# Cross attention laid over the feed forward's 56 slots, stage by stage

## The chip, the cores and the metric

One core of one Trainium2 chip runs the kernel. The metric is device time in microseconds (us), from one launch to its end. All data is float32.

## The reference

A transformer layer pair. An encoder layer runs over a context of 77 tokens (batch 2); a decoder layer runs over 2 x 2048 tokens of width 512 with 16 heads of 32: causal self attention, cross attention into the 77 encoder tokens, and a feed forward of width 2048. Both attentions add a learned bias by relative position. Cut to what matters here:

```python
y = y + _mha(yn, yn, dec_sa_in_w, dec_sa_in_b, dec_sa_out_w, dec_sa_out_b, sb)
y = y + _mha(_ln(y, dec_n2_s, dec_n2_b), memory, dec_ca_in_w, dec_ca_in_b, dec_ca_out_w, dec_ca_out_b, cb)
h = _ln(y, dec_n3_s, dec_n3_b)
y = y + (jax.nn.relu(h @ dec_ff1_w.T + dec_ff1_b) @ dec_ff2_w.T + dec_ff2_b)
```

## The kernel before

The decoder's tokens are cut into 8 blocks of 512 (`blocks`, four for each batch entry), a block into 4 tiles of 128 tokens, t = 0 to 3. The kernel has two phases. In the first, self attention of all blocks runs, the encoder and the cross attention of block 0 mixed in between. It writes each block's rows to a buffer in device memory (`y1`). The second phase, which the change touches, does the feed forward of block x and, beside it, the cross attention of block x + 1.

**The feed forward.** Each of its two layers is cut into a 2 x 2 grid, and a product of the two grids is made from 7 products of sums and differences instead of 8 (`PARTS`, `ORDER`). Each of these is done in four quarters, so a block has 2 x 7 x 4 = 56 *slots*, `per` in the code: 28 of layer 1, then 28 of layer 2. `ff_slot(s)` first issues the operands of slot s + 3 (`prepare`, L1061: sums of weights and of inputs on GpSimd, sums of hidden values on VectorE in layer 2), then the matmuls of slot s: `first_product` (L1078) in layer 1, `second_product` (L1108) in layer 2. A slot is 4 float32 matmuls that the trace lists as 8. Four PSUM banks (4 to 7) take their results. In layer 1 VectorE copies them (L1090) or adds them (L1094) into the hidden values `kT`, ScalarE copies a part (L1092) and applies the relu (L1097). In layer 2 VectorE adds every fourth slot's result to the block's rows (L1116); finished rows are stored (L1121), and rows of the block after next are loaded into their place (`new_y`, L962).

**Cross attention.** `cross(x)` is a generator: it fills lists of functions, `plan`, and gives control back after each list. Four other PSUM banks, handed out in rotation by `bank()`, serve it. Its stages for a tile t, and the lines of their instructions:

- the second norm, three stages: statistics on VectorE (L699 to L701) with an inverse root on GpSimd (L702); centring on VectorE into `xt` (L708) and, on GpSimd, adding the output's bias to the residual rows (L709); transposes on TensorE (L714) with scale and shift alternating on VectorE (L720) and ScalarE (L718)
- the queries, four groups for all four tiles at once (L727, evicted at L728 on VectorE)
- `score`: 16 heads' products on TensorE (L741) into four banks, then maxima and differences on VectorE (L750, L751) into one buffer `pr`, the program's `oT`; where a bias is added (block 4's tiles 0 and 1), `bias` has loaded it into `pr` before (L106), and L748 adds it
- `exp` on ScalarE (L754)
- `normalize`: sum and reciprocal on VectorE (L759, L760), a multiply on GpSimd (L761)
- `turned`: 16 transposes on TensorE (L767) into the four banks, copied by ScalarE (L771) and VectorE (L769) in turn
- `times_v`: the product with the values (L778), copied by ScalarE into `xr` (L782)
- `out`: the output product (L787), added to the rows by VectorE (L788)
- the third norm, the same three stages as the second (L699 to L720), which writes the feed forward's input `nTt`

**What sets the order.** Every engine works through its own instructions in the order in which the program issues them, so a wait holds whatever stands behind it on that engine. The loop at the end issues, for each slot n, the lists of `plan` that are due, then `ff_slot`. Before the change `plan` has 32 lists, *steps*, spread over the 56 slots:

```python
while steps < n * 32 // per + 1:
    next(side, None)
    steps += 1
```

So step s comes ahead of slot ceil(1.75 s): steps 0, 1, 2, 3, 4 ahead of slots 0, 2, 4, 6, 7, and so on, every four steps seven slots. The first block's slots 0 to 7 have been done before this loop, so its steps there have no matmuls of the feed forward beside them. The last block has no cross attention beside it. Within a list the functions stand by tile, the earlier tile first.

Of the kernel before, what the change touches and what calls it, by code (L numbers as in the profile page):

```python
# [54 lines left out]
def tile_encoder_decoder(ctx: ExitStack, tc: tile.TileContext, ins, out):  # L55
# [22 lines left out]
    def vec(name, i):  # L78
        c = _COL[name] + i
        return vecs[:, c : c + 1]  # L80
# [18 lines left out]
    def bias_tile(dst, m, nq, nk, off):  # L99

        flat = tz[m].rearrange("h b t -> h (b t)")
        for r0 in range(0, nq, RB):
            n = min(RB, nq - r0)
            o = off - r0
            skew = flat[:, o : o + RB * (LT - 1)].rearrange("h (b u) -> b h u", u=LT - 1)
            nc.sync.dma_start(dst[r0 : r0 + n], skew[:n, :, :nk])  # L106
# [43 lines left out]
    with (  # L150
# [20 lines left out]
        def bank():  # L171

            i = count["bank"] % count["banks"]
            count["bank"] += 1
            return psum[:, i, :]
# [515 lines left out]
        def norm_stages(y, n, row, place, done):  # L691

            keep = {}

            def stats():
                st = sm.tile([P, 6], F32, name="bnst", tag="bnst")
                mv = sm.tile([P, 2], F32, name="cmv", tag="cmv", bufs=4)
                rs = sm.tile([P, 2], F32, name="crs", tag="crs", bufs=4)
                nc.vector.bn_stats(st, y())  # L699
                nc.vector.bn_aggr(mv, st)  # L700
                nc.vector.tensor_scalar_add(rs[:, 0:1], mv[:, 1:2], EPS)  # L701
                nc.gpsimd.tensor_tensor(rs[:, 1:2], rs[:, 0:1], mhalf[:, 0:1], ALU.pow)  # L702
                keep.update(mv=mv, rs=rs)

            def center():
                xn = keep["xn"] = place()
                mv, rs = keep["mv"], keep["rs"]
                nc.vector.tensor_scalar(xn, y(), mv[:, 0:1], rs[:, 1:2], ALU.subtract, ALU.mult)  # L708
                nc.gpsimd.tensor_tensor(y(), y(), row, ALU.add)  # L709

            def turned():
                xn, pt, dst = keep["xn"], bank(), done()
                for c in range(NC):
                    nc.tensor.transpose(pt[:, ts(c, P)], xn[:, ts(c, P)], ident)  # L714
                for c in range(NC):
                    sc, bi = vec(f"dec_{n}_s", c), vec(f"dec_{n}_b", c)
                    if c % 2:
                        nc.scalar.activation(dst[:, c, :], pt[:, ts(c, P)], AF.Identity, bias=bi, scale=sc)  # L718
                    else:
                        nc.vector.tensor_scalar(dst[:, c, :], pt[:, ts(c, P)], sc, bi, ALU.mult, ALU.add)  # L720

            return stats, center, turned

        def q_group(o, w, nT, dst):
            mm = bank()
            for c in range(NC):
                nc.tensor.matmul(mm, w[:, c, :], nT[:, c, :], start=(c == 0), stop=(c == NC - 1))  # L727
            nc.vector.tensor_scalar(dst, mm, vec("dec_ca_in_b", o), SCALE, ALU.add, ALU.mult)  # L728
# [138 lines left out]
        for x, (b, m) in enumerate(blocks):  # L867
# [14 lines left out]
            for t in range(TB):  # L882
                end = x == len(blocks) - 1
                jobs[u + NU + (2 if end else 7) + t].append(out_job(b, m, t))
                at = u + NU + ((-1, 0, 3, 4)[t] if end else 6 + t)
# [6 lines left out]
            for g in range(NC):  # L892
# [3 lines left out]
                at = u + g * TB - 3  # L896
# [48 lines left out]
        nT2 = vflat[:, 12 * D :].rearrange("p (c n) -> p c n", n=MB)  # L945
        pr = oT_all.rearrange("p a q -> p (a q)")[:, : H * S]
        kTcs = [pts_all[:, 4 + b, : NC * S].rearrange("p (c k) -> p c k", k=S) for b in range(B)]
        w_q, vcs, qT = [], [], []
# [7 lines left out]
        def y_of(x, t):  # L956
            return ys[x % 2][:, t, :]
# [177 lines left out]
        def ff_slot(s):  # L1135
            prepare(s + 3)
            (first_product if slots[s][1] == 1 else second_product)(s)

        def cross(x):

            b, m = blocks[x]
            plan = [[] for _ in range(32)]

            def place(tag):
                return lambda: sb.tile([P, D], F32, name=tag, tag=tag, bufs=3 if tag == "xt" else 2)

            def bias(t):
                bias_tile(pr.rearrange("p (h k) -> p h k", k=S), 2, P, S, 255 - P * t)

            for t in range(TB):  # L1150
                fs = norm_stages(
                    lambda t=t: y_of(x, t), "n2", bv, place("xt"), lambda t=t: nT2[:, :, ts(t, P)]
                )
                for k, f in enumerate(fs):
                    plan[t + k].append(f)
            for g in range(NC):
                plan[6 + g // 2].append(lambda g=g: q_group(g, w_q[g], nT2, qT[g // 2][:, g % 2, :]))
            for t in range(TB):
                at = 8 + 4 * t
                y = lambda t=t: y_of(x, t)  # L1160
                biased = m == 0 and t < 2
                if biased:
                    plan[at if t else at - 2].append(lambda t=t: bias(t))
                fs = attend_stages(
                    lambda g, t=t: qT[g // 2][:, g % 2, ts(t, P)], kTcs[b], vcs[b], y, biased, pr,
                    lambda g: pts_all[:S, g, :], place("xr"), wbt,
                )
                for k, f in zip((0, 1, 2, 4, 5, 6), fs):
                    plan[at + k].append(f)
                fs = norm_stages(y, "n3", bo, place("xt"), lambda t=t: nTt[:, :, ts(t, P)])  # L1170
                for k, f in enumerate(fs):
                    plan[at + 7 + k].append(f)
            for fs in plan:
                for f in fs:
                    f()
                yield
# [40 lines left out]
        per = len(slots) // len(blocks)  # L1217
        for x in range(len(blocks)):
            side = cross(x + 1) if x + 1 < len(blocks) else iter(())
            steps = 0  # L1220
            for n in range(per):
                while steps < n * 32 // per + 1:
                    next(side, None)
                    steps += 1
                if x or n >= 8:
                    ff_slot(x * per + n)

# [36 lines left out]
```

## Time and profile before

| | |
|---|---|
| median of 3 runs | 3166.06 us (3164.92 to 3169.56) |
| the profiled execution | 3163.36 us |
| its span, first to last instruction | 3161.5 us |
| mean granted TensorE clock | 0.978 of full |
| TensorE busy | 3007.3 us, 95% |
| VectorE busy | 2052.0 us, 65% |
| ScalarE busy | 1379.0 us, 44% |
| GpSimd busy | 740.8 us, 23% |
| the phase of the change | from about 1914 us to the end |

Shares of busy time are of the whole span, both phases. In the rows below, PE is TensorE's matmuls, PEld its weight loads, DVE VectorE, ACT ScalarE, POOL GpSimd and SP the engine that issues DMAs. A group or chain row names a line of the program (L1108), what is written and read, and a time. A row of waits reads: who waited, for whom, us in total, times, the longest. A row of windows reads: start and end, length, then busy time of PE, PEld, DVE, ACT and POOL with instruction counts, the granted TensorE clock (1.00 is full), the share of busy DMA engines and GB/s.

### The profile page before, as it was taken

What the parts mean: (1) busy time and instruction counts of PE and PEld (TensorE: products, weight loads), DVE (VectorE), ACT (ScalarE), POOL (GpSimd) and SP (SyncE); (2) the same over time, 40 slices, a digit from 0 to 9 for tenths busy, and PEclk for the clock granted to TensorE, in tenths of its full rate; (3) what the DMA queues carried; (4) which work ended last, traced back from release to release, by engine and by line L of the source; (5) the groups of instructions that cost most, each with busy time, mean ns of one, the idle gap of its engine ahead of it and who ended that gap; (6) DMA issues with size and microseconds to landing.
All of it is one profiled execution on the core that took longest, in us unless ns stands there. A gap on an engine that the chain in (4) does not pass through costs nothing. (4 is left out here: it accounts for less than half of the span.)

```text
span 3161.5 us, 60599 instructions
## 1 busy us (share of the span) xinstructions
PE 3007.3 (95%) x24328; PEld 2066.4 (65%) x24328; DVE 2052.0 (65%) x5859; ACT 1379.0 (44%) x2523; POOL 740.8 (23%) x601
## 2 busy tenths in 40 slices
PE   7899999999999999999999989999999899999999
PEld 4555566666665556666666656777777677777778
DVE  4765667766765777667666645566666666666665
ACT  3443456667775445566677752122121212121211
POOL 0100000000000101000000014464545364646355
PEclk9899999999999999999999999999999999999999
DMA  5413201101114312212010222000001000000000
GB/s 154 106 43 117 79 21 48 55 22 38 32 35 95 94 32 70 67 38 61 19 35 12 61 82 104 1 27 1 27 1 35 9 27 1 27 1 27 1 14 14
DMA packets 117643, 137.10 MB, mean 43 GB/s; under 512 B 18240, under 2 KB 73072, under 8 KB 117234
## 3 DMA queue, kind: packets, MB, share of 16 engines
q1 hardware_dynamic: 117362, 133.22, 14.4%
q8 instruction: 192, 3.15, 0.4%
q14 instruction: 89, 0.73, 0.1%
HBM read 111.33 MB, written 21.86 MB: 42 GB/s over the span
## 5 line engine op out<-in xcount | busy, mean ns | idle before, releaser
L352 DVE TENSOR_SCALAR_CACHE_REDUCE pp<-psum 128x512 f32<-128x512 f32 (+3 forms) x1024 | 560.5, 589 | 290.8 <-PE psum L343 290.8
L367 ACT ACTIVATE pp<-pp,nm 128x128 f32<-128x128 f32 (+15 forms) x512 | 610.5, 1194 | 152.7 <-DVE nm L366 149.9
L393 ACT COPY pts<-psum 128x512 f32<-128x512 f32 (+3 forms) x816 | 408.3, 581 | 427.6 <-PE psum L387 418.8
L387 PEld LDWEIGHTS psum<-ident,pp 128*128 128x128 f32 x4352 | 480.0, 141 | 120.6 <-issue 97.6
L387 PE MATMUL psum<-ident,pp 128*128 128x128 f32 x4352 | 543.4, 276 | 15.0 <-ACT pp L367 12.0
L1061 POOL TENSOR_TENSOR vv<-pp 128x512 f32<-128x512 f32 x320 | 422.5, 1337 | 192.8 <-PE psum L1078 128.5
L406 PEld LDWEIGHTS psum<-pts,vv 128*32 128x32 f32 x8704 | 219.3, 110 | 270.3 <-issue 145.4
L343 PE MATMUL psum<-kT,q 32*128 32x512 f32 (+3 forms) x2560 | 381.4, 577 | 4.0 <-ACT kT L219 0.8
L406 PE MATMUL psum<-pts,vv 128*32 128x128 f32 x8704 | 342.0, 279 | 30.6 <-DVE pts L391 27.8
L359 DVE CUSTOM_DVE_ANT_0 pp<-psum,bias 128x256 f32<-128x256 f32 (+1 forms) x512 | 209.7, 410 | 60.1 <-PE psum L343 60.0
L1097 ACT ACTIVATE kT<-kT,vecs 128x256 f32<-128x256 f32 x256 | 114.4, 499 | 301.4 <-DVE kT L1094 301.4
L391 DVE COPY pts<-psum 128x512 f32<-128x512 f32 (+3 forms) x328 | 195.5, 644 | 43.8 <-PE psum L387 42.8
L267 POOL TENSOR_TENSOR rstd<-rstd,mhalf 128x1 f32<-128x1 f32 x32 | 18.4, 575 | 876.8 <-DVE rstd L266 876.8
L1094 DVE TENSOR_TENSOR kT<-kT,psum 128x512 f32<-128x512 f32 x256 | 166.1, 679 | 56.5 <-PE psum L1078 56.3
L343 PEld LDWEIGHTS psum<-kT,q 32*128 32x128 f32 x2560 | 135.0, 183 | 80.5 <-issue 45.2
L1108 PE MATMUL psum<-vv 128*128 128x256 f32 x768 | 178.3, 387 | 0.0
L252 POOL TENSOR_TENSOR xr<-xr,row_dec_sa_out_b 128x512 f32<-128x512 f32 x32 | 40.7, 1273 | 544.9 <-DMA xr<-in_x_dram 414.5
L1108 PEld LDWEIGHTS psum<-vv 128*128 128x128 f32 x768 | 148.6, 195 | 29.7 <-issue 9.5
L1078 PE MATMUL psum<-oT,vv 128*128 128x256 f32 x736 | 166.8, 380 | 0.0
L718 ACT ACTIVATE nT<-psum,vecs 128x128 f32<-128x128 f32 x56 | 25.6, 457 | 319.0 <-DVE nT L720 319.0
L1061 DVE TENSOR_TENSOR vv<-kT 128x512 f32<-128x512 f32 x160 | 157.8, 1007 | 8.9 <-PE psum L1108 8.0
L1078 PEld LDWEIGHTS psum<-oT,vv 128*128 128x128 f32 x736 | 139.3, 190 | 25.2 <-issue 6.7
(162 smaller groups left out, 4096.7 us busy)
## 6 DMA issues: line engine op xcount, KB each, us to landing
wqk<-in_dec_sa_in_wT_dram SPq DMA_DIRECT2D x64, 256.0 KB, 4.2
bias<-tz SPq DMA_DIRECT2D x128, 128.0 KB, 3.4
wbig<-in_dec_sa_in_wT_dram SPq DMA_DIRECT2D x8, 1024.0 KB, 7.5
vv<-in_enc_ff_wT_dram SPq DMA_DIRECT2D x8, 1024.0 KB, 5.3
wbig<-in_dec_sa_out_wT_dram SPq DMA_DIRECT2D x8, 1024.0 KB, 8.2
xr<-in_x_dram SPq DMA_DIRECT2D x32, 256.0 KB, 3.0
y<-xr SPq DMA_DIRECT2D x32, 256.0 KB, 2.8
vv<-y SPq DMA_DIRECT2D x32, 256.0 KB, 3.2
```

What stands on the lines that cost most here:

```text
L343: nc.tensor.matmul(banks[r][:, : kn * P], q[rows4(r), ts(t, P)], kT[rows4(r), g, k0 * P : (k0 + kn) * P], start=True, stop=True,)
L352: nc.vector.tensor_scalar(p[:, k0 * P : (k0 + far) * P], s[:, : far * P], 1.0, None, ALU.mult, ALU.max, accum_out=st["mx"][:, r, c : c + 1],)
L359: nc.vector.tensor_tensor_reduce(p[:, (i + 1) * P - w : (i + 1) * P], s[:, far * P : kn * P], biases[b, m, g][:, r, 2 * P - w :], 1.0, LOW ...
L367: nc.scalar.activation(p[:, : (i + 1) * P], p[:, : (i + 1) * P], AF.Exp, bias=nm, accum_out=sums_of[b, m, g][:, t, r : r + 1],)
L387: nc.tensor.transpose(pt[:, ts(x, P)], p[r][:, ts(k0 + k, P)], ident)
L391: nc.vector.tensor_copy(pts[:, : len(group), :], pt[:, :w])
L393: nc.scalar.copy(pts[:, : len(group), :], pt[:, :w])
L406: nc.tensor.matmul(ot[rows4(r), t, :], vv[:, k0 + k, ts(g * HC + r, HD)], got[r, k], start=(k0 + k == 0), stop=(k0 + k == nb - 1),)
L1061: engine.tensor_tensor(dst, quarter(*parts[0], n), quarter(*parts[2], n), SIGN[parts[1]])
L1078: nc.tensor.matmul(mm[:, ts(f, TOK)], a[:, c, ts(f, P)], b[:, c, :], start=(c == 0), stop=(c == 1))
L1094: nc.vector.tensor_tensor(dst, dst, got, SIGN[sign])
L1108: nc.tensor.matmul(mm[:, t, :], lhs[:, c, ts(t, P)], rhs[:, c, :], start=(n == 0 and c == 0), stop=(n == 3 and c == 1),)
```

## The change

`plan` gets one list for each slot, 56 in all, and the loop takes one list per slot. The stages' places are written in slots. The second norm's three stages of tile t go to t, t + 2 and t + 4; the four query groups to 9, 10, 11 and 12; tile t's attention starts at 14 + 7t with its six stages at +0, +2, +3, +6, +9 and +11; the third norm's three stages follow at +13, +15 and +17. The bias of tile 0 is loaded four slots ahead of its scores, that of tile 1 in the scores' own list, as before.

In slots, the places before and after are these (tile t's attention starts at 14 + 7t in both):

| stage | before | after |
|---|---|---|
| second norm, statistics, t = 0 to 3 | 0, 2, 4, 6 | 0, 1, 2, 3 |
| second norm, centring | 2, 4, 6, 7 | 2, 3, 4, 5 |
| second norm, transposes | 4, 6, 7, 9 | 4, 5, 6, 7 |
| queries, four groups | 11, 11, 13, 13 | 9, 10, 11, 12 |
| score, exp | +0, +2 | +0, +2 |
| normalize | +4 | +3 |
| turned | +7 | +6 |
| times_v, out | +9, +11 | +9, +11 |
| third norm, statistics | +13 | +13 |
| third norm, centring | +14 | +15 |
| third norm, transposes | +16 | +17 |

```diff
--- before.py
+++ after.py
@@ -1139,7 +1139,7 @@
         def cross(x):
 
             b, m = blocks[x]
-            plan = [[] for _ in range(32)]
+            plan = [[] for _ in range(per)]
 
             def place(tag):
                 return lambda: sb.tile([P, D], F32, name=tag, tag=tag, bufs=3 if tag == "xt" else 2)
@@ -1151,25 +1151,25 @@
                 fs = norm_stages(
                     lambda t=t: y_of(x, t), "n2", bv, place("xt"), lambda t=t: nT2[:, :, ts(t, P)]
                 )
-                for k, f in enumerate(fs):
+                for k, f in zip((0, 2, 4), fs):
                     plan[t + k].append(f)
             for g in range(NC):
-                plan[6 + g // 2].append(lambda g=g: q_group(g, w_q[g], nT2, qT[g // 2][:, g % 2, :]))
+                plan[9 + g].append(lambda g=g: q_group(g, w_q[g], nT2, qT[g // 2][:, g % 2, :]))
             for t in range(TB):
-                at = 8 + 4 * t
+                at = 14 + 7 * t
                 y = lambda t=t: y_of(x, t)
                 biased = m == 0 and t < 2
                 if biased:
-                    plan[at if t else at - 2].append(lambda t=t: bias(t))
+                    plan[at if t else at - 4].append(lambda t=t: bias(t))
                 fs = attend_stages(
                     lambda g, t=t: qT[g // 2][:, g % 2, ts(t, P)], kTcs[b], vcs[b], y, biased, pr,
                     lambda g: pts_all[:S, g, :], place("xr"), wbt,
                 )
-                for k, f in zip((0, 1, 2, 4, 5, 6), fs):
+                for k, f in zip((0, 2, 3, 6, 9, 11), fs):
                     plan[at + k].append(f)
                 fs = norm_stages(y, "n3", bo, place("xt"), lambda t=t: nTt[:, :, ts(t, P)])
-                for k, f in enumerate(fs):
-                    plan[at + 7 + k].append(f)
+                for k, f in zip((13, 15, 17), fs):
+                    plan[at + k].append(f)
             for fs in plan:
                 for f in fs:
                     f()
@@ -1217,11 +1217,8 @@
         per = len(slots) // len(blocks)
         for x in range(len(blocks)):
             side = cross(x + 1) if x + 1 < len(blocks) else iter(())
-            steps = 0
             for n in range(per):
-                while steps < n * 32 // per + 1:
-                    next(side, None)
-                    steps += 1
+                next(side, None)
                 if x or n >= 8:
                     ff_slot(x * per + n)
 
```

## The prediction

> **What bounds the kernel.** I read the span, the seven feed-forward blocks that carry cross attention as windows, TensorE's waits in them, then the chain of waits of one block.
>
> ```profile
> core 0: 3161.5 us, clock 0.978
> ```
> ```profile
> 2234.09:2397.91 163.82, 154.53 (x865) 120.61 (x864) 105.58 (x180) 34.38 (x68) 83.75 (x66) 0.96 0.04 14
> 2397.91:2568.88 170.97, 155.12 (x865) 120.42 (x864) 110.16 (x188) 34.25 (x68) 83.94 (x66) 0.96 0.09 21
> 2250.80:2254.20 3.40, 3.40 (x10) 2.68 (x9) 2.87 (x7) 0.91 (x2) 2.50 (x3) 0.50 0.00 0
> 2342.90:2349.70 6.80, 6.67 (x37) 5.63 (x38) 4.93 (x12) 0.00 (x0) 2.67 (x3) 0.50 0.02 4
> 2374.00:2382.00 8.00, 6.36 (x22) 3.78 (x21) 3.61 (x7) 1.39 (x3) 1.55 (x2) 1.00 0.00 0
> 2455.00:2461.00 6.00, 4.47 (x53) 3.63 (x51) 4.85 (x8) 3.67 (x8) 5.91 (x5) 1.00 0.09 17
> ```
>
> The first two windows are whole blocks: 163.8 us for an ordinary one, 171.0 for the one beside which block 4 (with a bias) is prepared. TensorE is busy for 154.5 of 163.8 (second number), yet the seventh number, the granted clock, drops to 0.50 inside, so part of that busy time is slow work.
>
> ```profile
> PE psum L741 <- DVE pts L769: 32.7, 20, 2.4
> PE psum L787 <- ACT xr L782: 15.3, 8, 3.7
> PE psum L714 <- DVE xt L708: 14.8, 7, 2.2
> PE psum L741 <- ACT pts L771: 2.9, 7, 0.4
> PE psum L767 <- POOL oT L761: 2.8, 7, 1.5
> ```
>
> These are TensorE's own waits from 1920 us to the end (total, times, longest). Counts of 7 are once a block. Where they sit shows in the chain of the block from 2234:
>
> ```profile
> 2248.86 0.46 DVE xt L708
> 2249.37 0.66 PE psum L714 x4
> 2250.03 5.14 PE psum L1078 x16
> 2255.17 0.44 PE psum L714 x4
> 2255.61 3.46 PE psum L1078 x16
> 2259.06 6.87 PE psum L727 x16
> ...
> 2277.98 1.06 PE psum L741 x32
> ...
> 2287.46 1.36 DVE csu L759
> 2289.24 2.26 POOL oT L761
> 2291.54 1.97 PE psum L767 x16
> ...
> 2314.38 0.52 POOL crs L702
> 2314.93 1.48 DVE xt L708
> 2316.40 1.21 DVE pts L769 x2
> 2317.65 1.11 PE psum L741 x26
> 2318.76 5.34 PE psum L1108 x16
> 2324.10 0.44 PE psum L714 x4
> 2324.54 1.01 PE psum L778 x32
> ...
> 2356.11 3.43 PE psum L787 x8
> 2359.55 5.18 PE psum L1108 x24
> 2364.73 1.75 PE psum L767 x16
> ```
>
> The undisturbed pieces price the block's TensorE work: 56 slots at 1.73 (16 matmuls, two slots, in 3.46) are 96.9; queries 2 x 6.87 = 13.7; eight norm transposes at 0.44, 3.5; four times scores 1.06, transposed probabilities 1.75, values 1.01 and output 3.43, 29.0. Together 143.1. The block takes 163.8, so 20.7 us are lost, at five places:
>
> - A, slot 7: the transposes of token tile 2 (L714) wait for its centring on VectorE: 14.8/7 = 2.1. The two slots behind run at half clock: 5.14 for 3.46, 1.7 more.
> - B, slot 21: transposed probabilities wait for GpSimd's normalisation, about 0.4 (2.8/7).
> - C and D, slots 28 and 35: scores wait for the bank copies of the transposes that precede them in the same step: (32.7 + 2.9)/7 = 5.1. The clock halves behind each: 1.9 in C (5.34 for 3.46), and D's 6.8 us at 0.50 cost up to 3.4.
> - E, slot 46: output waits for ScalarE's copy: 15.3 less the biased block's 3.7, over seven, 1.7.
>
> That is 16.3; the other 4.4 are restarts after waits, which wait rows leave out, and small gaps. TensorE is the bound, VectorE's order is why it waits. In C the reader sees how: GpSimd's rsqrt (L702), VectorE's centring (L708, 1.48), and only then the two bank copies (L769), all in one step.
>
> **The change, part by part.** Step s of 32 ran at the slot ceil(1.75 s). So scores stood at 14 + 7t already, with exp +2, values +9, output +11 and the third norm's statistics +13; these keep their slots. Six things move. I follow each on the queues.
>
> *The three stages that met.* At slots 21, 28 and 35 one step held the centring of n3(t-2), the transposes of t-1 and the scores of t. Now the transposes go one slot earlier (+6), the centring one later (+15). Between the last transpose and the first score TensorE does a slot of 1.73, and the centring is behind both on VectorE. For t = 1, counted from scores(0) at 0 with B's wait: output(0) ends at 28.5, slots 25 and 26 end at 32.0, transposes run 32.0 to 33.7, slot 27 to 35.5. VectorE has slot 26's addition, n3's statistics (about 1.1, below), then two copies (1.21), done near 35.1. Scores(2) want the banks at 35.5: no wait, margin 0.4. For t = 2 the same count leaves 0.7. So C goes, 1.9 of half clock with it, and D's.
>
> *Normalisation one slot earlier (+3).* Exp keeps its slot, so VectorE can now stand still for it, and the feed forward's evictions stand behind.
>
> ```profile
> L754 ACT ACTIVATE oT<-oT x4: 1215/1235/1240, 2285.0 to 2353.7; 128x1232 f32<-128x1232 f32 x4
> ```
>
> In the block shown exp(0) starts at 2285.0 and ends near 2286.2. VectorE's sum over it (L759), at 2287.46 before, can start there, 1.2 earlier, since slot 17's two additions move behind it; VectorE stands still for at most that. GpSimd is then done 1.2 earlier too, at 2290.4, while the transposes are wanted a slot earlier, at 2289.4 (2291.54 less 0.4 of wait less 1.73). B's wait grows from 0.4 to 1.0; its scores, a slot apart from the copies, stop waiting. Slot 17's additions come 1.8 later; four feed-forward banks are three slots, 5.2, of cover. For t = 1 to 3 normalisation now precedes the output's VectorE addition, and GpSimd is done 2.4 or more ahead of need. GpSimd's operand additions queue behind it; by the same count slot 20's is there 0.5 early.
>
> *Values ahead of the third norm's transposes.* These now come at +17, values at +9, so they part company. E's ScalarE copy stood behind L718; now it does not. E goes. The norm's own transposes have two slots behind the centring; in slot 38 I count 0 to 0.3 of wait and take 0.2. The last one is at slot 52 instead of 51, and GpSimd reads it for the next block from slot 53 for use at 56, two slots of cover.
>
> *The first norm: statistics in slots 0 to 3 instead of 0, 2, 4, 6, transposes in 4 to 7 instead of 4, 6, 7, 9, queries one each in 9 to 12 instead of two each in 11 and 13.* VectorE carries this.
>
> ```profile
> L1090 DVE COPY kT<-psum 128x512 f32<-128x512 f32 x8 | 5.5, 686 | 2.4 <-ACT kT L1092 2.4
> L1094 DVE TENSOR_TENSOR kT<-kT,psum 128x512 f32<-128x512 f32 x5 | 3.4, 680 | 0.8 <-PE psum L1078 0.8
> L699 DVE BATCH_NORM_STATS2 bnst<-vv 128x6 f32<-128x512 f32 x4 | 2.7, 686 | 0.0
> L720 DVE TENSOR_SCALAR vv<-psum,vecs 128x128 f32<-128x128 f32 x6 | 2.4, 405 | 1.6 <-ACT vv L718 1.6
> L708 DVE TENSOR_SCALAR xt<-vv,cmv,crs 128x512 f32<-128x512 f32 x4 | 2.1, 537 | 0.0
> ```
> ```profile
> 2237.13 2.10 SPq L962 DMA_DIRECT2D vv<-y  x2
> ```
> ```profile
> DMA to landing us min/median/max: 3.0/3.1/3.2
> ```
>
> Statistics with aggregate and epsilon are about 1.1 each, 4.4; centrings 2.1; eight L720 3.2 and four waits of 0.53 for ScalarE between them 2.1; evictions of slots 0 to 6, ten at 0.64, 6.4; VectorE starts 0.9 late behind the last block. One wait is new: the loads of tiles 2 and 3 are issued from 2237.1 to 2239.2 and land 3.1 after their issue, the first 6.2 into the block. Statistics of tile 2 now come up at 5.4: 0.8. Sum 19.9. TensorE reaches the queries after nine slots and 4 x 0.44, 17.3. So it waits 2.6 in all, in pieces of under 1 at tiles 2 and 3, slot 8's operand (GpSimd behind L709) and the queries. Bounds: nothing, if tiles overlap better; A's 3.8 again, if the clock halves. I take 2.6, without half clock: the window 2374 to 2382 holds E's pause of 1.7 at a clock of 1.00, and these pieces are smaller.
>
> *The bias of block 4* loads one slot earlier for t = 0 (hidden either way) and after its transposes for t = 1. VectorE's chain is longer there by the additions, so the wait at slot 20 is 3.3 against 1.5: 1.7 worse, once. The output's 3.7 behind the bias DMA stays.
>
> **The sum.** Waits left per block: 2.6 + 1.0 + 0.2 = 3.8; with 1.3 of small gaps 143.1 + 5.1 = 148.2 against 163.8: 15.6 less. Six blocks 93.6, minus 1.7; the first block has no A (its first eight slots have no matmuls, ±1) and gains about 14. In all 106: span 3161.5 to 3055.5, profiled run 3163.4 to 3057.4. The median of the runs is 2.7 above that execution: 3060.
>
> **The rivals.**
> 1. The clock halves in the first norm all the same: 7 x 1.7 = 12, 3072. For it: A's 2.2 was enough. Against it: E's 1.7 was not. Chance 0.10.
> 2. A run of transposes with a wait halves the clock at slot 20, where 1.0 of wait and 1.75 of transposes stand together: 7 x 1.7 = 12, 3072. Against it: the window 2455 to 2461 has the longest wait of L767, 1.5, and a run of transposes (1.97 in the chain above) behind it, at 1.00. Chance 0.05. The Trainium skill, TensorE: Matmul & The Clock Gate, Part 4: PE-mode transpose, says that transposes do not count as TensorE activity in the same way; by that rule this rival holds, and the trace speaks against it.
> 3. One of the scores still waits: VectorE's copies now stand behind n3's statistics, with margins of 0.4 and 0.7. If C stays: half of L741's 5.1, a restart of 1.0 and its half clock of 1.9, 5.4 x 7 = 38, 3098. Chance 0.12.
> 4. The first norm's waits vanish too: 7 x 2.6 = 18 less, 3042. Chance 0.08.
> 5. No change to measure: attention kept nearly all its slots, and what waits is the VectorE work as such, so the waits reappear elsewhere: 3160. Against it: VectorE is busy 105.6 of 163.8. Chance 0.03.
> 6. Slower: normalisation holds VectorE for exp and evictions close the feed-forward banks. Price: the biased block's held VectorE costs 3.7 at one wait and 7.2 in all (171.0 less 163.8); 5.4, the middle, at each of 28 places is 151, 3211. It decides from 106/28 = 3.8 each; my count gives VectorE a pause of 1.2 and the banks 5.2. Chance 0.05.
>
> **Numbers.** The forecast, 3060, has 0.57. The range 3038 to 3100 takes in rivals 1 to 4 (0.92 with the forecast, less what a size missed takes). Within 0.2% is about what a measurement of this kernel can tell. Faster 0.92, same 0.03, slower 0.05.
>
> **What would show it.** Right: L741's waits for L769 near zero; L787's for L782 only in the biased block; two of three 0.50 stretches per block gone, or all; blocks of 148. L714 waiting for L708 and L727 for L720 in pieces below 1 confirm the first norm; L767 waiting about 1.0 for L761 once a block, slot 20. Wrong: a long wait of L741 for L769 behind L699, half clock at slots 7 to 9 or 20, or L1108 or L1078 waiting for VectorE's evictions.

## The result and the profile after

| | before | after |
|---|---|---|
| median | 3167.81 us (4 runs) | 3057.31 us (4 runs, 3054.33 to 3058.80) |
| profiled execution, its span | 3163.36, 3161.5 us | 3056.45, 3054.6 us |
| mean granted TensorE clock | 0.978 | 0.990 |

The ratio of the times is 0.965, with a 95% interval of 0.9633 to 0.9666: 3.5% faster. Windows of the kernel after, as they were read before: the block from 1882 (the first, which starts at its slot 8), an ordinary block, the one beside which block 4 is prepared, and a stretch inside that one.

```profile
1881.91:2056.63 174.72, 165.93 (x900) 124.46 (x901) 106.42 (x184) 34.73 (x68) 86.81 (x68) 0.95 0.16 53
2204.11:2351.64 147.53, 145.43 (x865) 113.43 (x864) 101.58 (x180) 34.83 (x68) 83.94 (x66) 1.00 0.04 15
2351.64:2509.15 157.51, 149.18 (x866) 115.44 (x864) 106.37 (x188) 34.94 (x68) 83.98 (x66) 0.98 0.09 22
2410.00:2413.20 3.20, 3.20 (x14) 3.02 (x13) 1.59 (x3) 1.61 (x4) 3.20 (x4) 0.50 0.01 3
```

An ordinary block went from 163.8 to 147.5 us, and its clock from 0.96 to 1.00: the three half-clock stretches are gone. The biased block went from 171.0 to 157.5. It is the only block behind the first that still has half clock, twice 3.4 us; the last row is one of these stretches. The first block of the kernel before, for comparison:

```profile
1882.14:2070.26 188.12, 173.59 (x901) 130.58 (x902) 109.01 (x184) 34.38 (x68) 86.57 (x68) 0.93 0.14 50
```

TensorE's own waits in the kernel after, from 1920 us on (total, times, longest):

```profile
PE psum L767 <- POOL oT L761: 8.1, 7, 3.2
PE psum L714 <- DVE xt L708: 6.9, 9, 1.6
PE psum L714 <- ACT vv L718: 3.7, 6, 0.6
PE psum L787 <- ACT xr L782: 3.2, 1, 3.2
PE psum L1078 <- DVE kT L1094: 0.5, 1, 0.5
```

L741's waits, 35.6 us in all before, are gone, and L787 waits once, in the biased block. The chain that ended last shows slots 25 to 35 of an ordinary block, where C (slot 28) and D (slot 35) were:

```profile
2274.83 3.45 PE psum L1078 x16
2278.29 1.75 PE psum L767 x16
2280.03 1.73 PE psum L1078 x8
2281.76 1.06 PE psum L741 x32
2282.82 3.65 PE psum L1108 x16
2286.47 1.01 PE psum L778 x32
2287.49 1.92 PE psum L1108 x8
2289.41 0.44 PE psum L714 x4
2289.85 1.73 PE psum L1108 x8
2291.57 3.43 PE psum L787 x8
2295.01 3.45 PE psum L1108 x16
2298.46 1.75 PE psum L767 x16
2300.21 1.73 PE psum L1108 x8
2301.94 1.06 PE psum L741 x32
```

It is TensorE throughout, each stage within 0.2 us of its undisturbed row. What is left stands in the second norm and at slot 20, in the same chain (two stretches of it):

```profile
2218.97 0.08 POOL vv L709
...
2220.20 1.29 POOL vv L1061
2221.49 0.04 issue
2221.53 1.99 PE psum L1078 x8
...
2256.02 2.26 POOL oT L761
2258.28 0.04 issue
2258.33 1.97 PE psum L767 x16
```

Slot 8's matmuls start when GpSimd has done the slot's operand (L1061), which stands behind the last addition to the rows (L709). Slot 20's transposes start when GpSimd's first normalisation is done.

### The profile page after: what moved, and what is told of

Read it like the earlier page. It is cut to its first block, busy times and chain, and to the rows that moved or that the text cites. A ratio compares the mean times of both kernels' runs of the same rounds, so it can differ in the third digit from the quotient of the medians.

```text
span 3054.6 us, 60599 instructions
## 1 busy us (share of the span) xinstructions
PE 2950.7 (97%) x24328; PEld 2020.6 (66%) x24328; DVE 2029.6 (66%) x5859; ACT 1382.6 (45%) x2523; POOL 739.6 (24%) x601
## 5 line engine op out<-in xcount | busy, mean ns | idle before, releaser
L1061 POOL TENSOR_TENSOR vv<-pp 128x512 f32<-128x512 f32 x320 | 418.3, 1324 | 150.2 <-PE psum L1078 130.5
L1061 DVE TENSOR_TENSOR vv<-kT 128x512 f32<-128x512 f32 x160 | 137.8, 879 | 9.9 <-PE psum L1108 8.9
L207 PE MATMUL psum<-nT,wqk 128*128 128x512 f32 x256 | 120.8, 616 | 0.5 <-DVE nT L289 0.5
```

Source lines behind the costliest of these rows:

```text
L1061: engine.tensor_tensor(dst, quarter(*parts[0], n), quarter(*parts[2], n), SIGN[parts[1]])
```

## Experiments

The theory was that C and D came from the order on VectorE: the bank copies stand behind the centring in one list. The rival was distance: transposes and scores share four banks, so in one list the scores wait whatever stands first. Spans are of profiled executions; each ratio is to the kernel before.

**Order alone, in the kernel before.**

```diff
-                    plan[at + 7 + k].append(f)
+                    (last if k == 1 else plan)[at + 7 + k].append(f)
...
-            for fs in plan:
+            for fs in (plan[k] + last[k] for k in range(32)):
```

> The kernel before, with one thing changed: in each step the third norm's centring stands last, behind the transposes of the probabilities and the scores, instead of first. No stage changes its step or slot. Theory (VectorE's order): the scores' long waits at slots 28 and 35 are the two bank copies standing behind the centring, which waits for GpSimd; with the copies ahead, each wait falls to the bank turnover that slot 21 shows (about 0.8 us), and the clock no longer halves there: 10.7 us less in each of seven blocks, 75 in all, span about 3087. The waits at slots 7 and 46 stay. Rival (distance): transposes and scores in one step share four banks, so the scores wait whatever stands first; only the centring's own 1.5 us at two places goes, 21 in all, span about 3140.

Measured: span 3095.1, ratio 0.9772 (0.9758 to 0.9787). 66 of the 107 us came without moving a stage to another slot. TensorE's waits:

```profile
PE psum L714 <- DVE xt L708: 23.1, 19, 2.2
PE psum L787 <- ACT xr L782: 3.7, 1, 3.7
PE psum L741 <- DVE pts L769: 3.7, 9, 0.5
PE psum L741 <- ACT pts L771: 2.9, 7, 0.4
```

L741's waits for L769 fell from 32.7 to 3.7. The span is 8 us over the forecast. The norms' transposes wait longer for the centring that now stands later (14.8 to 23.1). And transposes and scores in one list still take 3.8, 3.9 and 4.5 us together at slots 21, 28 and 35, where the undisturbed rows give 2.8 (1.75 and 1.06): distance has a part too, about 1 us or more at each of these slots. E's wait, which was to stay, went in the ordinary blocks, though the values and the third norm's transposes still shared a list: that list alone does not make it.

**Transposes back, centring back, both back**, in the kernel after:

```diff
-                for k, f in zip((0, 2, 3, 6, 9, 11), fs):
+                for k, f in zip((0, 2, 3, 7, 9, 11), fs):
```
```diff
-                for k, f in zip((13, 15, 17), fs):
+                for k, f in zip((13, 14, 17), fs):
```

> The kernel after, with the transposes of the probabilities moved back to +7, the slot of the next tile's scores; the centring stays at +15. Theory (VectorE's order): the scores wait about 0.8 us for the banks at slots 21, 28 and 35, the wait of 1.0 at slot 20 goes, so 1.4 more per block, 10 in all, span about 3065, no half clock. Rival (distance): the waits of 3 to 4 us and the half clock at slots 28 and 35 return, 80 in all, span about 3135.

> The kernel after, with the third norm's centring moved back to +14, the list of the scores, ahead of them; the transposes of the probabilities stay at +6. Theory (VectorE's order): the bank copies stand a slot ahead, so the centring delays only the scores' maxima; TensorE waits no more than before, span 3054 to 3058. Rival (distance): the same. A third view, that the early centring itself stalls VectorE for GpSimd's inverse root wherever it stands, gives 1 to 2 us at two slots, 14 to 28 in all, span 3068 to 3083.

> The kernel after, with both moved back: transposes of the probabilities at +7 and centring at +14, so that one list again holds centring, transposes and scores in this order; all else as after. Theory (VectorE's order): the long waits at slots 28 and 35 return with their half clock, 10 us per block, 70 in all, span about 3125, far more than the sum of the two single moves (10 and 0). Rival (distance): no more than the transposes' move alone.

Measured: 3089.3 (0.9755, 0.9741 to 0.977), 3055.5 (0.964, 0.9624 to 0.9656), 3095.6 (0.9773, 0.9758 to 0.9787). The centring's place alone costs nothing, as expected. The other two missed. The transposes' move cost 35, not 10. At the scores the forecast was near: transposes and scores take 3.7 to 3.9 us in most blocks instead of 2.8, at three slots about 3.1 per block where 2.4 was forecast. What it missed is TensorE's largest wait:

```profile
PE psum L1078 <- POOL oT L1061: 16.8, 7, 4.4
```

That is slot 20's operand, which GpSimd makes behind the early normalisation. In the kernel after, TensorE does the transposes meanwhile; with them a slot later it stands. Half clock follows in three of the six blocks without a bias. Both moves together cost 41, not 70, so order on VectorE is not the whole of C and D. One part of the change that concerns them is still in both runs: the early normalisation.

**The two other cases.** Normalisation back at +4, with the transposes at +7 and the centring at +14 (three back) or +15 (two back):

```diff
-                for k, f in zip((0, 2, 3, 6, 9, 11), fs):
+                for k, f in zip((0, 2, 4, 7, 9, 11), fs):
```

> The kernel after, with the transposes of the probabilities at +7, the centring at +14 and the normalisation at +4, so that attention stands as in the kernel before up to the third norm's transposes. Theory, mended after the run with two moves back: the long waits need both, the copies behind the centring, and the normalisation at +4, which fills GpSimd just before the inverse root that the centring waits for. So they return now: L741 waits for L769 about 4.8 us per block, the clock halves behind it, and slot 20's waits go: 8 to 10 per block, 56 to 70 in all, span 3110 to 3125. Rival: the early normalisation has no part in it, span as with the two moves back, 3090 to 3097.

> The kernel after, with the transposes of the probabilities at +7 and the normalisation at +4; the centring stays at +15. It completes the four cases of centring and normalisation with transposes at +7. Theory: with the centring away the late GpSimd costs nothing at the scores, so 0.8 us of bank turnover at three slots remains; slot 20's operand is ahead of the normalisation on GpSimd again, so the 2.3 and more of the single move goes; a wait of about 0.4 at slot 21 stays: 2.8 less 1.0 per block, 13 in all, span 3063 to 3070. Rival: late normalisation costs the scores whatever the centring does, span over 3095.

Measured: 3145.3 (0.9939, 0.9923 to 0.9956) and 3077.5 (0.9721, 0.9707 to 0.9736). The four cases, all with transposes at +7:

| span, us | centring +15 | centring +14, ahead of the copies |
|---|---|---|
| normalisation +3 | 3089.3 | 3095.6 |
| normalisation +4 | 3077.5 | 3145.3 |

The early centring costs 6 with the early normalisation and 68 with the late one. VectorE's waits show why: the centring's wait for GpSimd's inverse root, from 1960 us on, with three moves back, then with the early normalisation (3095.6), then with the late centring (3077.5).

```profile
DVE xt L708 <- POOL crs L702: 39.9, 28, 2.9
```
```profile
DVE xt L708 <- POOL crs L702: 9.3, 21, 0.4
```
```profile
DVE xt L708 <- POOL crs L702: 3.1, 7, 0.4
```

The kernel before has the first row word for word. There, at slot 28 of the block from 2234, GpSimd does the normalisation from 2309.68 and two operands behind it; the inverse root, whose input is ready at 2312.3, starts at 2314.3. So two things must meet: the normalisation late enough to fill GpSimd just ahead of the inverse root, and the copies behind the centring that waits for it. The row of TensorE's waits in the worst case closes the chain:

```profile
PE psum L741 <- DVE pts L769: 32.3, 17, 2.4
```

The span is 20 over the upper end of the forecast, likely because I had priced the half clock too low. By the records of the granted clock it holds for 99 us behind 1940 us, in 15 stretches; in the kernel before for 96. Two back misses by 8: slots 28 and 35 lose 1.1 and 1.7 from start to start, not 0.8, and slot 21 1.3. In one of its blocks the clock halves behind slot 35, though no pause there is over 0.5 us:

```profile
2776.30:2779.70 3.40, 3.40 (x10) 2.68 (x9) 3.30 (x8) 0.00 (x0) 0.00 (x0) 0.50 0.00 0
```

Ahead of this stretch stand 16 transposes and 32 scores, with pauses of half a microsecond and less, 4.5 us in all. The run with the order alone has the same at slot 35 of three blocks. At slot 35 of the other blocks, as long, the clock stays at 1.00 in both runs.

**The second norm and the queries back** (statistics 0, 2, 4, 6 and so on, queries at 11 and 13):

```diff
-                for k, f in zip((0, 2, 4), fs):
-                    plan[t + k].append(f)
+                for k, f in zip(((0, 2, 4), (2, 4, 6), (4, 6, 7), (6, 7, 9))[t], fs):
+                    plan[k].append(f)
...
-                plan[9 + g].append(lambda g=g: q_group(g, w_q[g], nT2, qT[g // 2][:, g % 2, :]))
+                plan[11 + g // 2 * 2].append(lambda g=g: q_group(g, w_q[g], nT2, qT[g // 2][:, g % 2, :]))
```

> The kernel after, with the second norm and the queries back in their former slots (statistics 0, 2, 4, 6, centring 2, 4, 6, 7, transposes 4, 6, 7, 9, queries two each at 11 and 13). Theory: the wait of 2.2 us at slot 7 and 1.7 of half clock behind it return in six blocks and the waits of about 1.9 that replaced them go: 2.1 per block more, 13 in all, span about 3067. Rival: with the other stalls gone VectorE comes to the norm less late, so nothing returns, span 3043 to 3055.

Measured: 3063.7 (0.968, 0.9665 to 0.9694), 9 more instead of 13. The wait returns in each of the six blocks, the half clock behind it in four. Two stretches with the same wait in two of the blocks, one without and one with:

```profile
2067.00:2077.00 10.00, 7.83 (x42) 6.51 (x41) 8.80 (x21) 2.29 (x5) 6.38 (x7) 1.00 0.01 2
2221.60:2225.00 3.40, 3.40 (x11) 2.78 (x9) 2.81 (x8) 0.86 (x2) 2.60 (x3) 0.50 0.02 5
```

So a pause of 2.2 us is at the edge: the same pause halves the clock or does not. In the kernel before it did in all six blocks, with the order alone in one of six.

**The third norm's transposes back at +16:**

```diff
-                for k, f in zip((13, 15, 17), fs):
+                for k, f in zip((13, 15, 16), fs):
```

> The kernel after, with the third norm's transposes moved back to +16, the list that holds the next tile's product with the values, ahead of it; the centring stays at +15. Theory (ScalarE's order): the copy of the values' product stands behind the norm's shift again, and output waits at slot 46 for it: up to 1.7 per block, 12 in all; and the transposes now have one slot behind the centring, which VectorE does behind the scores' maxima at slots 29 and 36: 1 to 2 more. Span 3060 to 3075. Rival (the wait at slot 46 came from VectorE's backlog, not from the shared list): span 3053 to 3058.

Measured: 3086.4 (0.975, 0.9735 to 0.9764), 32 more, over both forecasts:

```profile
PE psum L714 <- DVE xt L708: 29.1, 23, 2.5
```

Every block's cost is at slots 30 and 37, where the transposes now wait for a centring that VectorE does behind the scores' maxima one slot before: about 1.0 and 2.8, some with half clock. L787 still waits for L782 only in the biased block. So the shared list alone does not bring E back; the two slots between centring and transposes are worth 32 us.

**Normalisation back at +4**, transposes at +6:

```diff
-                for k, f in zip((0, 2, 3, 6, 9, 11), fs):
+                for k, f in zip((0, 2, 4, 6, 9, 11), fs):
```

> The kernel after, with the normalisation moved back to +4; the transposes stay at +6. Theory: at slot 20 TensorE's wait grows from 1.0 to about 2.7 and at the others GpSimd is still ahead or late by under 1: 12 to 20 in all, span 3067 to 3075 without half clock. A wait of 2.7 followed by 1.75 of transposes also tests the clock: if a wait of over 2.1 us halves it, as at slot 7 of the kernel before, or if transposes do not count as activity, 1.7 per block more, span 3079 to 3087.

Measured: 3099.5 (0.9784, 0.9767 to 0.98), 45 more, over both forecasts: the cost is at all tiles, not at the first alone.

```profile
PE psum L767 <- POOL oT L761: 45.6, 28, 3.2
```
```profile
2267.80:2275.30 7.50, 5.55 (x36) 4.50 (x34) 5.08 (x8) 3.09 (x7) 5.95 (x5) 1.00 0.00 0
2744.70:2748.10 3.40, 3.40 (x17) 3.40 (x18) 0.69 (x1) 1.30 (x3) 3.40 (x3) 0.50 0.02 5
```

GpSimd is late by 1.6 in the mean at 28 places. The window from 2267.8 is slot 20 of one block, a pause of 2.0 and 1.8 of transposes in one stretch, at full clock. So it is in five of the six blocks without a bias. In the sixth the same pause is followed by 3.4 us at half clock, from 2744.7, and the transposes take 3.5.

**Three tries for a faster version.**

```diff
-                for k, f in zip((0, 2, 4), fs):
+                for k, f in zip((0, 2, 4 if t < 2 else 5), fs):
...
-                plan[9 + g].append(lambda g=g: q_group(g, w_q[g], nT2, qT[g // 2][:, g % 2, :]))
+                plan[10 + g].append(lambda g=g: q_group(g, w_q[g], nT2, qT[g // 2][:, g % 2, :]))
...
-                at = 14 + 7 * t
+                at = 15 + 7 * t
+                first = -1 if t == 0 else 0
...
-                for k, f in zip((0, 2, 3, 6, 9, 11), fs):
+                for k, f in zip((first, first + 2, first + 3, 6, 9, 11), fs):
```

> A version that may beat both: the kernel after, with the second norm's transposes at 4, 5, 7, 8, queries at 10 to 13, and all attention from tile 0's transposes on one slot later (15 + 7t), while tile 0's scores, exp and normalisation keep slots 14, 16 and 17. Theory: VectorE gets one more slot before the queries (waits of 1.8 in the norm go), GpSimd's first normalisation one more slot before its transposes (1.0 goes): 2.8 per block, 18 in all, span about 3037. Rival: the waits move to the block's end, where the last transposes of the third norm now stand at slot 53 and the next block's inputs wait for them: span 3050 to 3060.

```diff
+                early = 1 if t == 0 else 0
...
-                for k, f in zip((0, 2, 3, 6, 9, 11), fs):
+                for k, f in zip((-early, 2 - early, 3 - early, 6, 9, 11), fs):
```

> The kernel after, with tile 0's scores, exp and normalisation one slot earlier (13, 15, 16); its transposes and all else stay. Theory: the normalisation has one more slot before slot 20 and no longer stands ahead of slot 20's operand: the wait of 1.04 goes in seven blocks and 1.7 more in the biased one, 9 in all, span about 3046. Rival: VectorE, which does the scores' maxima in slot 13 among the last query's eviction and slot 12's, comes late with the feed forward's evictions instead: span 3052 to 3058.

```diff
-                nc.gpsimd.tensor_tensor(y(), y(), row, ALU.add)
+                if not apart:
+                    add_row()
+            def add_row():
+                nc.gpsimd.tensor_tensor(y(), y(), row, ALU.add)
...
-                for k, f in zip((0, 2, 4), fs):
+                for k, f in zip((0, 2, 4, 9), fs):
```

> As the run before, and GpSimd's addition of the output's bias to the rows in the second norm (L709) stands in slots 9 to 12 instead of behind each centring in slots 2 to 5. Theory: GpSimd's operand for slot 8 is then there in time and the inverse roots are not behind it: the wait at slot 8, 0.4, goes, and of the waits at tiles 2 and 3, 1.4, which are VectorE's, up to half, because VectorE shares nothing with GpSimd there: 0.4 to 1.0 per block, 3 to 6 in all, span 3040 to 3043. Rival: the additions delay GpSimd's operands in slots 9 to 15 instead: no gain, span 3046 or more.

Measured: 3070.8 (0.9702, 0.9687 to 0.9716), 3068.5 (0.9703, 0.9688 to 0.9717), 3074.8 (0.9728, 0.9713 to 0.9743). All three are slower than the kernel after, and none of my rivals had the reason. In all three it is once more an operand behind the normalisation (17.0, 16.7 and 16.7 us of wait), and in the first slot 8's operand too (10.6), behind L709; TensorE's wait with tile 0 early:

```profile
PE psum L1078 <- POOL vv L1061: 16.7, 7, 4.4
```

From the scores to GpSimd's start of the first normalisation it takes 10.1 us in the kernel after (2245.89 to 2256.02) and 10.2 with tile 0 early: the chain over VectorE and ScalarE sets it, not the list. A slot earlier in the list only puts another operand, slot 19's, behind it. In the third, the additions gone from slots 2 to 5 let GpSimd make its operands there without a break, and VectorE's centring beside it slows. The group of the second norm in the third try, then in the kernel after:

```profile
L708 DVE TENSOR_SCALAR xt<-vv,cmv,crs 128x512 f32<-128x512 f32 x4 | 5.1, 1282 | 0.0
```
```profile
L708 DVE TENSOR_SCALAR xt<-vv,cmv,crs 128x512 f32<-128x512 f32 x4 | 3.1, 780 | 0.0
```

The waits at tiles 2 and 3 grow from 0.6 and 0.8 to 1.6 and 1.7 per block. The Trainium skill, GPSIMD Engine Reference, 1. Specifications, says that GpSimd shares its SBUF interfaces with VectorE and contends with some of its instructions; the trace agrees, with 0.54 us for a centring beside an idle GpSimd and 1.5 beside a busy one; no run shows whether the centring is one of the instructions that the page means. What these three point to, tile 0's scores and exp a slot earlier with the normalisation left at slot 17, was not tried.

## Why the prediction was right, point by point

*C and D go.* They did, wholly: 5.1 of wait and all of their half clock per block. But the reason was half told. The prediction put it on the copies behind the centring and took the normalisation's move as a cost alone; the four cases show that either the late centring or the early normalisation removes most of it, and that both old places together make it.

*E goes.* It did, and the step that gave the reason, ScalarE's copy behind L718 in a shared list, is one half of it. Slot 46 in the kernel before, from the chain:

```profile
2374.39 0.33 DVE nT L720
...
2375.68 0.46 ACT nT L718
2376.14 0.48 ACT xr L782
2376.63 0.04 issue
2376.67 1.55 PE psum L787 x3
```

The copy (L782) stands behind L718, and L718 waits for L720, which VectorE does late: at slot 42 its centring has stood 2.9 us for the inverse root. Where the list is shared and VectorE is not late, L787 waits in the biased block alone (order alone, and the third norm's transposes back). Where VectorE is as late but the list is not shared, it does so too: that is the run with three moves back, whose centring has the same 39.9 us of waits, and TensorE's row there is:

```profile
PE psum L787 <- ACT xr L782: 3.7, 1, 3.7
```

So two things must meet here as well, and the prediction named one. (That run differs from the kernel before also in the second norm and the queries, some 30 slots away.)

*Normalisation earlier.* The wait of 1.0 at slot 20 was measured as 8.1 less the biased 3.2 over six blocks, 0.8 by the wait rows (1.0 from start to start). The 0.4 of B was a mean that holds the biased block's 1.5; the other six share 1.3. The operand at slot 20, said to be there early, is so only because the transposes cover it; without this cover it is 16.8 of the 35 us that the transposes' move back cost. The prediction did not price that cover. Nor did it price what moving the normalisation is worth, 45 us with the transposes at +6: it is one half of what lets them go a slot earlier.

*The second norm.* Forecast 2.6 per block; from start to start of TensorE's work 0.6, 0.8 and 0.4, 1.8. The sum of VectorE's work held, 19.7 us from the block's start at 2204.11 to the last L720, against 19.9, but partly by luck. L708, taken at 0.54, is 0.78 in the mean, 1.0 more for four; and the wait of 0.8 for the loads of tiles 2 and 3, which was to come once a block, came to 1.6 in two places of the phase, 1.4 of it in the one ordinary block that took 148.9 us. The queries do not wait for the last transposes at all; their piece was the over-sized term. VectorE's wait for the loads in the kernel after:

```profile
DVE bnst L699 <- DMA vv<-y: 1.6, 2, 1.4
```

*Slot 38.* Forecast 0.2, measured none.

*The biased block.* Forecast 1.7 worse than the others; it gained 13.5 where an ordinary one gained 16.3, so 2.8 worse. The wait at slot 20 is 3.2 and the clock halves behind it, which the sum left out.

*The sum.* The five ordinary blocks gained 14.9 to 16.4, 16.0 in the mean, instead of 15.6; the first 13.4 (188.1 to 174.7) instead of 14, the biased one 13.5 instead of 13.9: span 3054.6 against 3055.5 forecast. That it is within 1 us is luck in part: terms of up to 1 us per block were off both ways.

*The clock.* Rivals 1 and 2 did not come: no pause of TensorE in an ordinary block of the kernel after is over 0.9 us. The rule of the Trainium skill quoted with rival 2, that transposes do not count as activity in the same way, is left open. A pause of 2.0 followed by 1.8 of transposes kept the clock at 1.00 in five blocks of six, where pauses of 2.2 with 0.5 of transposes halved it in six, four and one of six; but at slot 35, behind transposes and scores, it halved four times with no pause over 0.5.

## What to carry to other kernels

When one engine is the bound, price its work from its undisturbed rows and call the rest loss; then follow each loss back through the in-order queues to the two things that meet there, since moving either may be enough. A move is worth what stands behind it in its queue as much as its own wait: the normalisation one slot earlier is worth 45 us here, and costs 16.8 of waits for one operand as soon as the work that covered it moves. Distance counts by the pair: here the third norm's transposes needed two slots behind the centring on VectorE (one cost 32 us), and those of the probabilities three behind the normalisation on GpSimd (two cost 45).

## What the runs showed of the hardware

- A TensorE pause of 2.2 us was followed by 3.4 us at half clock in six of six like places of the kernel before, in four of six with the second norm back and in one of six with the order alone; a pause of 2.0 with 1.8 of transposes behind it in one of six. Pauses of 1.7 in the kernel before left the clock at 1.00.
- The clock also halved with no pause over 0.5 us, behind 4.5 us of transposes and scores, in one of seven like places with two moves back and in three of seven with the order alone. So pauses are not all that counts.
- A VectorE centring of 128x512 takes 0.54 us beside an idle GpSimd and about 1.5 beside one that computes, so taking work away from GpSimd's critical stretch and letting it run ahead made VectorE slower there (0.78 to 1.28 in the mean).
